# Loads behind the edge exchange, and larger pieces of filler work, in a lattice-and-convolution kernel

## The chip, the core and the metric

The kernel runs on one core of a Trainium2 chip. The metric is the device time of one execution in microseconds (us): 12252.35 us in the median of three runs, from 12244.07 to 12260.76. One more execution was recorded by the hardware profiler; its rows are what the text quotes. Of the core's engines, TensorE (PE, PEld for its weight loads) multiplies matrices, VectorE (DVE), ScalarE (ACT) and GpSimd (POOL) work elementwise, and SyncE (SP) only issues transfers (DMAs), in the order of its queue.

## What is computed

The input x has 32 images of 8 channels of 256 x 256. Two residual layers follow each other:

```python
# layer 0, v = groupnorm(x)
drive = grid = v
for _ in range(15):
    mapped = 3.9 * grid * (1.0 - grid)
    local = conv3x3(mapped, K_local, groups=8)         # each channel for itself
    grid = 0.85 * (0.7 * mapped + 0.3 * local) + 0.15 * drive
cml = clip(grid, 1e-4, 1 - 1e-4)
nca = sigmoid(conv1x1(relu(conv3x3(v, Wp, bp)), Wu, bu))       # 8 -> 128 -> 8 channels
g = sigmoid(conv1x1(relu(conv3x3(concat(v, cml, nca), Wg1, bg1)), Wg2, bg2))
x = x + g * cml + (1 - g) * nca
# layer 1, v = groupnorm(x): both sides quantised to whole numbers up to 127
x = x + conv3x3(q(v), q(weight)) / (sx * sw) + bias
```

## The kernel before

The images are worked on in 8 groups of 4. Layer 0 of a group has four kinds of work, all with TensorE at their centre.

*The lattice* (`lattice`, `half`) iterates `grid`. One channel of four images is a unit; a unit's four images are two pairs, s = 0 and s = 1, and each of the 15 steps does s = 0 and then s = 1. One such piece, 32 matrix products in 64 x 64 quarters of the array and three tiny marks between them (lines 502 and 277), is called a *stretch* here; there are 8 x 8 x 15 x 2 = 1920. A stretch writes two PSUM units; VectorE then takes each half out (`gt`, line 513) and applies the map (line 523), which makes the next step's operand, `m_a` or `m_b`, in SBUF. The image lies over the partitions in overlapping tiles, so that after some steps the rows at the tiles' edges must come from neighbours. Where step + s is even, the stretch reads `m_a`, writes `m_b`, and a small GpSimd product mends the edge (line 528). Where it is odd, it reads `m_b`, writes `m_a`, and two transfers from `m_a` to `m_a` carry the edge rows, 33 KB each: the *exchange* (lines 477 and 478, on SyncE's queue). The next stretch of the same pair s, two stretches later, reads what the exchange brings. No exchange is made in the last step.

*The hidden layer* (`nca`, line 588) makes 128 channels from 8. One *ph pair* is 12 matrix products into one PSUM unit; ScalarE applies the relu (line 596). The 1 x 1 product that follows is the *acc* work: four products at a time (line 604). An image is done in 8 bands t, each with 8 ph pairs and four times four acc products, from an input tile `im` that four transfers of 384 KB fill (line 569), for the next band while this one runs; there are two `im` buffers.

*The gate* (`gate`, line 767) does per band 4 products with the last band's result (line 717) and 40 with two tiles `gin` and `gnc` (three transfers of 384 KB), and takes a third input, `mix` (two transfers of 384 KB, one buffer), to the elementwise end on GpSimd and VectorE. It runs one group behind.

*The preparation* (`normalise`) of the next group's images is small on TensorE.

TensorE's order is that of the program. `together` lays it: after each stretch it takes pieces from the other three kinds, the filler, until the filler's share of its total weight has caught up with the lattice's. The weights are what the generators yield: 2.05 for a stretch, 1.4 for a ph pair, 0.9 for four acc products, 2.3 for a gate batch; the totals stand in `T_NCA`, `T_GATE`, `T_PREP`, `T_LATTICE` (line 896). After each stretch one of the gate's elementwise steps (`chores`) is written too, among them the request for the next `mix`. The other engines and SyncE's queue are ordered by a scheduler with its own estimate of times: a load may be put into the queue anywhere that its buffer and its place in the program allow. All transfers of layer 0 go through SyncE's queue; apart from the loads named above these are the drive's pieces for the next unit (`d_a`, `d_b`, 36 KB and more), the lattice's results, the normalised images and the outputs of hidden layer and gate.

PSUM has three units of two banks for stretches (two each), ph pairs (one) and gate batches (one).

After the last group's lattice and hidden layer come its gates alone, and then layer 1, which the change doesn't touch.

Of the kernel before, what the change touches and what calls it, by code (L numbers as in the profile page):

```python
# [31 lines left out]
F32 = mybir.dt.float32  # L32
# [77 lines left out]
def kernel(  # L110
# [19 lines left out]
    def dram_ap(t, offset, dims):  # L130
        return bass.AP(t.tensor, t.offset + offset, dims)
# [123 lines left out]
    with ExitStack() as one:  # L255
# [139 lines left out]
        def lattice(g):  # L395
# [67 lines left out]
            def background(n):  # L463
# [4 lines left out]
                if g == 0 and units.keys() - {0}:  # L468
                    for _ in range(min(n, len(borders))):
                        nc.sync.dma_start(*borders.pop(0))  # L470

            def exchange(t):

                t = t.rearrange("p (k t) j -> p k (t j)", k=2)
                n = (NT - 1) * (NJ + 2)
                above, below = slice(0, n), slice(NJ + 2, NJ + 2 + n)
                nc.sync.dma_start(t[0::16, :, below], t[14::16, :, above])
                nc.sync.dma_start(t[15::16, :, above], t[1::16, :, below])
# [4 lines left out]
            def half(c, step, s, d, m_a, m_b):  # L483

                a2b = (step + s) % 2 == 0
                n = NJ + 1 if a2b else NJ
                k = 0 if a2b else 1
                two = [unit(), unit()]

                def blocks(j, diagonal, first):  # L490
                    t0, t1 = JOBS[j]
                    pt = two[j // 2][:, j % 2, : (t1 - t0) * n].rearrange("p (t j) -> p t j", j=n)
                    own = m_a[:, t0:t1, 1 : 2 + NJ] if a2b else m_b[:, t0:t1, 0:NJ]
                    beside = m_a[:, t0:t1, 0 : 1 + NJ] if a2b else m_b[:, t0:t1, 1 : 1 + NJ]
                    if diagonal:
                        parts = ((LOW, LOW, k, own), (HIGH, HIGH, k, own))
                    elif a2b:
                        parts = ((LOW, HIGH, k, own), (HIGH, LOW, 2, beside))
                    else:
                        parts = ((HIGH, LOW, k, own), (LOW, HIGH, 2, beside))  # L500
                    for src, dst, w, rhs in parts:
                        T.matmul(pt[dst], lw[src, c, w, dst], rhs[src], start=first, stop=not first)  # L502

                for n_, (o, dg, first) in enumerate(((1, 0, True), (3, 2, True), (0, 1, False), (2, 3, False))):
                    blocks(o, False, first)
                    blocks(dg, True, first)
                    if n_ < len(MARKS):
                        mark(n_)

                gts = []  # L510
                for pt, (ts, w) in zip(two, HALVES):
                    gt = gp.tile([P, 10 * (NJ + 1)], F32, name="gt", tag="gt")[:, : 2 * w * n]
                    V.scalar_tensor_tensor(  # L513
                        gt.rearrange("p (u c) -> p u c", u=2), pt[:, :, : w * n], FLOOR,
                        d[:, ts, :].rearrange("p (u t) j -> p u (t j)", u=2), ALU.max, ALU.add,
                    )
                    gts.append(gt.rearrange("p (t j) -> p t j", j=n))
                for gt, (ts, w) in zip(gts, HALVES):
                    if step == STEPS - 1:
                        V.tensor_scalar(d[:, ts, :], gt, 0.0001, 1.0 - 0.0001, ALU.max, ALU.min)  # L520
                        continue
                    to = m_b[:, ts, :] if a2b else m_a[:, ts, 1 : 1 + NJ]
                    V.scalar_tensor_tensor(to, gt, 1.0, gt, ALU.subtract, ALU.mult)  # L523
                if step == STEPS - 1:
                    return a2b
                if a2b:
                    edge = m_b[:, :, 0 : NJ + 1 : NJ]
                    G.tensor_tensor(edge, edge, junk.unsqueeze(1).to_broadcast([P, TU, 2]), ALU.mult)  # L528
                else:
                    exchange(m_a)  # L530
                return a2b

            if g == 0:
# [5 lines left out]
            for c in range(C):  # L539
                u = g * C + c  # L540
                for step in range(STEPS):
                    if step == 7 and u + 1 < NG * C:
                        units[u + 1], dmas = load(u + 1)
                        later.extend(dmas)
                    if step == STEPS - 1:
                        background(len(later))
                    for s in range(2):
                        d = units[u][s][1 if (step + s) % 2 == 0 else 0]
                        a2b = half(c, step, s, d, m_a[s], m_b[s])
                        if step == STEPS - 1:  # L550
                            for k in range(2):
                                later.extend(store(g * GB + 2 * s + k, c, "b" if a2b else "a", d, k))
                            if u + 1 in units:
                                begin(units[u + 1], s)
                        background(4)
                        yield 2.05

            stored[g] = issued[0] + len(later)
            if g == NG - 1:
                background(len(later))  # L560

        ORDER = ((0, 4, 1, 5), (2, 6, 3, 7))

        def rows(b, t):

            im = ims[(NT8 * b + t) % 2]
            for k in range(2):
                for q in range(2):
                    nc.sync.dma_start(
                        im.bitcast(F32)[64 * q : 64 * q + 48, k, :, 1 : 1 + W],  # L570
                        dram_ap(
                            xp_s[b % NBUF], (32 * t + 16 * k + 8 * q) * ROW, [[W, 48], [ROW, 8], [1, W]]
                        ),
                    )
            return im

        loaded = {}

        def nca(b):
# [19 lines left out]
            pend = done = None  # L599

            def drain():
                acc, t, i, hs = pend
# [20 lines left out]

            ahead = loaded.pop(b, None) or rows(b, 0)
            for t in range(NT8):
                im = ahead
                acc = ps_a.tile([P, 512], F32, name="acc", tag="acc")
                for i in range(4):
                    hs = {}
                    for n in (i, i + 4):  # L630
                        hs[n], hs[n + 8] = hidden([im[64 * q : 64 * q + 48, :, n, :] for q in range(2)])
                        if n == 0:
                            if t < NT8 - 1:
                                ahead = rows(b, t + 1)
# [12 lines left out]
            nc.sync.dma_start(*done)  # L647

        def scales(b):
# [9 lines left out]
        def inputs(b, t):  # L659

            src = gs_s[b % NBUF]
            gin = gip.tile([96, 8, W], F32, name="gin", tag="gin")
            gnc = gip.tile([48, 8, W], F32, name="gnc", tag="gnc")
            for j, to in enumerate((gin[:48], gin[48:], gnc)):
                nc.sync.dma_start(
                    to, dram_ap(src, j * PART + 32 * t * C * W, [[W, 48], [4 * C * W, 8], [1, W]])
                )
            return gin, gnc

        def blend(b, t):  # L670

            src = gs_s[b % NBUF]
            mix = gip.tile([P, 3, 2, W], F32, name="mix", tag="mix", bufs=1)
            for k in range(2):
                nc.sync.dma_start(
                    mix[:, :, k, :],
                    dram_ap(src, (32 * t + 16 * k + 1) * C * W, [[W, P], [PART, 3], [1, W]]),
                )
            return mix

        flat = lambda t: t.rearrange("p k w -> p (k w)")

        def arrange(sc, mix):
# [24 lines left out]
        def gate(b):  # L708
# [38 lines left out]
            for t in range(NT8 + 1):  # L747
# [5 lines left out]
                    now["gt"] = opened(two[:, 1, :], last["r1"])  # L753
                    now["was"] = last
                if t < NT8:
                    (gin, gnc), mix = ahead
# [21 lines left out]
                    was["y"] = mixed(now["gt"], *was["df"])  # L778

                def arrange_(now):  # L780
                    now["df"] = arrange(sc, now["mix"])

                def blend_(now):
                    if now["t"] < NT8 - 1:
# [106 lines left out]
        def after(g, gen):  # L891
# [189 lines left out]
```

## Time and profile before

| | |
|---|---|
| profiled execution | 12231.09 us, of it 12229.3 us span |
| median of the runs | 12252.35 us |
| lattice with filler | to about 11,290 us of the span |
| last gates alone | to about 11,670 us |
| layer 1 | to the end |
| TensorE busy, 1500 to 11,000 us | 8830.18 of 9500 us, granted clock 0.98 |
| VectorE busy, same stretch of time | 6212.55 us |
| DMA engines' busy share, same | 0.70, at 141 GB/s |
| transfers | 1760 MB, of it 896 exchanges of two times 33 KB and 2304 loads of 384 KB |

A line of the page's groups reads: line, engine, operation, output<-inputs, form and count, then busy time and the mean of one in ns, then the idle time of the engine just before these instructions with what ended it. A line of the time order reads: start, duration, engine, line, operation, count, and in brackets the idle time before it with what ended it; PE is TensorE, and SPq is SyncE's queue, where the duration is the issue alone and says nothing of the landing. A line of the time windows reads: from:to, length, busy time (and count) of PE, PEld, DVE, ACT and POOL, then the granted TensorE clock, the DMA engines' busy share and GB/s.

### The profile page before, as it was taken

Reading aid. Unit: us, or ns where it says so; the run is one execution under the profiler, and the core shown is the slowest. Engines: PE = TensorE matmul, PEld = TensorE weight load, DVE = VectorE, ACT = ScalarE, POOL = GpSimd, SP = SyncE. Lnnn points to the kernel's source line nnn. Section 1 sums busy time; section 2 is a strip of 40 time slices with the busy share of each in tenths; the row PEclk is TensorE's granted clock in tenths of the full one; section 3 lists DMA queues with packets and bytes.
Section 4 is the critical chain, followed back from the end, with each engine's and each line's share of the span. In section 5 each row is a group of like instructions: output and inputs, shape, how many; then the busy total and the mean of one; then the engine's idle time right before and its main releaser. Section 6 shows DMA issues by size and latency. Waiting matters only on the chain. (4 is left out here: it accounts for less than half of the span.)

```text
span 12229.3 us, 289998 instructions
## 1 busy us (share of the span) xinstructions
PE 10809.9 (88%) x124192; PEld 6033.0 (49%) x124192; DVE 7826.2 (64%) x11376; ACT 3791.0 (31%) x4034; POOL 1577.2 (13%) x2242
## 2 busy tenths in 40 slices
PE   4888899999999999999999999999999999999854
PEld 2544555555555555555555555555555555554222
DVE  4655666666666666666666666666666666665377
ACT  2222233332333333333333333333333333332133
POOL 1000011111111111111111111111111111111200
PEclk7999999999999999999999999999999999999776
DMA  6545567766777667766776667777677666665988
GB/s 171 97 98 102 101 136 147 143 140 138 147 142 148 137 137 145 151 141 134 148 151 139 135 140 147 143 145 149 133 146 149 141 133 129 126 123 114 204 249 259
DMA packets 2473159, 1759.74 MB, mean 144 GB/s; under 512 B 1021280, under 2 KB 2442944, under 8 KB 2471744
## 3 DMA queue, kind: packets, MB, share of 16 engines
q1 hardware_dynamic: 2380096, 1651.64, 66.0%
q10 hardware_dynamic: 91776, 89.53, 2.3%
q8 instruction: 979, 16.04, 0.6%
q14 instruction: 308, 2.52, 0.1%
HBM read 1130.62 MB, written 473.89 MB: 131 GB/s over the span
## 5 line engine op out<-in xcount | busy, mean ns | idle before, releaser
L596 ACT ACTIVATE h<-pt,bp_sb 128x1024 f32<-128x1024 f32 x2048 | 2275.6, 1113 | 4947.7 <-PE pt L588 4944.3
L588 PE MATMUL pt<-im,wp_hi 48*128 48x512 f32 x12288 | 2631.8, 424 | 165.4 <-ACT h L596 116.6
L502 PE MATMUL pt<-m_a,lw 64*64 64x325 f32 (+1 forms) x30720 | 2299.3, 433 | 464.9 <-DMA m_a<-m_a 410.1
L513 DVE SCALAR_TENSOR_TENSOR gt<-pt,d_b 128x650 f32<-128x650 f32 (+1 forms) x1920 | 1463.5, 763 | 1945.0 <-PE pt L502 1931.7
L588 PE MATMUL pt<-im,wp_lo 48*128 48x512 f32 x12288 | 2442.5, 393 | 0.2 <-issue 0.2
L513 DVE SCALAR_TENSOR_TENSOR gt<-pt,d_a 128x640 f32<-128x640 f32 (+1 forms) x1920 | 1447.2, 754 | 1531.5 <-PE pt L502 1528.2
L502 PE MATMUL pt<-m_b,lw 64*64 64x320 f32 (+1 forms) x30720 | 2200.5, 417 | 118.1 <-DVE gt L513 82.1
L502 PEld LDWEIGHTS pt<-m_a,lw 64*64 64x64 f32 x30720 | 1316.6, 138 | 1193.2 <-issue 596.9
L588 PEld LDWEIGHTS pt<-im,wp_hi 48*128 48x128 f32 x12288 | 1163.6, 185 | 1275.4 <-issue 719.4
L502 PEld LDWEIGHTS pt<-m_b,lw 64*64 64x64 f32 x30720 | 1237.4, 134 | 858.4 <-issue 463.5
L523 DVE SCALAR_TENSOR_TENSOR m_a<-gt 128x640 f32<-128x640 f32 (+1 forms) x1792 | 1431.7, 799 | 58.6
L523 DVE SCALAR_TENSOR_TENSOR m_b<-gt 128x650 f32<-128x650 f32 (+1 forms) x1792 | 1384.6, 774 | 101.3 <-DVE gt L513 2.8
L528 POOL TENSOR_TENSOR m_b<-m_b,junk 128x36 f32<-128x36 f32 x896 | 243.8, 272 | 7994.9 <-DVE m_b L523 5672.1
L588 PEld LDWEIGHTS pt<-im,wp_lo 48*128 48x128 f32 x12288 | 1168.7, 186 | 201.7 <-issue 0.6
L604 PE MATMUL acc<-h,wu_z 128*32 128x512 f32 x8192 | 1107.7, 612 | 0.0
L767 PE MATMUL pt<-gin,gw 96*32 96x384 f32 (+2 forms) x10240 | 772.0, 450 | 201.3 <-ACT gate L719 178.0
L277 PE MATMUL mark<-qw 64*64 64x1 bf16 x5760 | 947.6, 165 | 0.0
L277 PEld LDWEIGHTS <-qw 64*64 64x64 bf16 x5760 | 632.4, 110 | 205.4 <-issue 9.8
L767 PE MATMUL pt<-gnc,gw 48*32 48x126 f32 (+2 forms) x10240 | 733.1, 429 | 0.0
L767 PEld LDWEIGHTS pt<-gin,gw 96*32 96x32 f32 x10240 | 313.8, 115 | 823.7 <-issue 425.2
L690 POOL TENSOR_TENSOR d<-mix 128x256 f32<-128x256 f32 x512 | 552.1, 1095 | 1240.8 <-DVE gate L725 840.1
L767 PEld LDWEIGHTS pt<-gnc,gw 48*32 48x32 f32 x10240 | 295.0, 108 | 420.8 <-issue 415.3
(110 smaller groups left out, 5939.0 us busy)
## 6 DMA issues: line engine op xcount, KB each, us to landing
im<-xp_s SPq DMA_DIRECT2D x1024, 384.0 KB
gin<-gs_s SPq DMA_DIRECT2D x512, 384.0 KB
mix<-gs_s SPq DMA_DIRECT2D x512, 384.0 KB
gnc<-gs_s SPq DMA_DIRECT2D x256, 384.0 KB
d_a<-gs_s SPq DMA_DIRECT2D x2048, 36.0 KB
yb<-y_s ACTq DMA_DIRECT2D x28, 2432.0 KB
xr<-in_x_dram SPq DMA_DIRECT2D x128, 512.0 KB
xp_s<-hi SPq DMA_DIRECT2D x256, 256.0 KB
```

Source lines behind the costliest of these rows:

```text
L277: T.matmul(one_[dst], qw[src, 0, dst], qw[src, 0, 0:1], start=True, stop=True)
L502: T.matmul(pt[dst], lw[src, c, w, dst], rhs[src], start=first, stop=not first)
L513: V.scalar_tensor_tensor(gt.rearrange("p (u c) -> p u c", u=2), pt[:, :, : w * n], FLOOR, d[:, ts, :].rearrange("p (u t) j -> p u (t j)", ...
L523: V.scalar_tensor_tensor(to, gt, 1.0, gt, ALU.subtract, ALU.mult)
L528: G.tensor_tensor(edge, edge, junk.unsqueeze(1).to_broadcast([P, TU, 2]), ALU.mult)
L588: T.matmul(ph[:, i, :].rearrange("p (h w) -> p h w", w=W), w[64 * i : 64 * i + 48, dx, :], rhs[:, :, dx : dx + W], start=(dx == 0 and w is ...
L596: S.activation(h.rearrange("p i c -> p (i c)"), ph.rearrange("p i c -> p (i c)"), AF.Relu, bias=bp_sb)
L604: T.matmul(acc[32 * g : 32 * g + 32], wu_z[:, 24 - 8 * i : 56 - 8 * i], hs[4 * g + i], start=(i == 0), stop=(i == 3),)
L690: G.tensor_tensor(d[:, cols], mix[:, 1, k], mix[:, 2, k], ALU.subtract)
L767: T.matmul(three[32 * i : 32 * i + 32, :, to], gw[:rows_, j, dx, :], src[:, i::4, of], start=(j == 0 and n == 0), stop=(j == 1 and n == le ...
```

## The change

Two things are changed. The large loads (`im`, `gin`, `gnc`, `mix`) are no longer issued where they are requested: a request goes into a list, `asked`. When a stretch makes an exchange, `feed` issues the oldest requests, until 1200 KB are spent (with 384 KB each, up to four), each with an ordering edge that puts it behind the exchange's second transfer in SyncE's queue. Whoever needs a tile whose load was not issued by then issues it himself (`settle`); after the last group's lattice there is no waiting for exchanges (`alone`).

And the filler comes in larger pieces: two ph pairs at a time (weight 2.9), eight acc products at a time after every second of these (1.9), a gate batch with weight 4.5, a stretch with 2.4; the totals follow. The number of products of each kind is the same.

```diff
+            def feed(behind):
+                room = 1200
+                while asked and room > 0:
+                    job = asked.pop(0)
+                    if job[1]:
+                        room -= job[0]
+                        tc.add_manual_dep(begun(job).ins, behind.ins.name, BEHIND, reason="behind the exchange")
+
             def exchange(t):
...
-                nc.sync.dma_start(t[15::16, :, above], t[1::16, :, below])
+                return nc.sync.dma_start(t[15::16, :, above], t[1::16, :, below])
...
-                    exchange(m_a)
+                    feed(exchange(m_a))
...
-                        yield 2.05
+                        yield 2.4
...
             if g == NG - 1:
                 background(len(later))
+                alone.append(True)
+                settle(asked)
...
+        asked, alone = [], []
+        BEHIND = mybir.DependencyInfo(mybir.DependencyClass.NoSync, mybir.DependencyReason.DATA)
+
+        def begun(job):
+            args, job[1] = job[1], None
+            return nc.sync.dma_start(*args)
+
+        def settle(jobs):
+            for job in jobs:
+                if job[1]:
+                    begun(job)
+
+        def ask(jobs):
+            if alone:
+                settle(jobs)
+            else:
+                asked.extend(jobs)
+            return jobs
...
             ahead = loaded.pop(b, None) or rows(b, 0)
             for t in range(NT8):
-                im = ahead
+                im, jobs = ahead
+                settle(jobs)
                 acc = ps_a.tile([P, 512], F32, name="acc", tag="acc")
                 for i in range(4):
                     hs = {}
                     for n in (i, i + 4):
                         hs[n], hs[n + 8] = hidden([im[64 * q : 64 * q + 48, :, n, :] for q in range(2)])
-                        if n == 0:
-                            if t < NT8 - 1:
-                                ahead = rows(b, t + 1)
-                            elif all((b + 1, g) in ready for g in range(4)):
-                                loaded[b + 1] = rows(b + 1, 0)
-                        yield 1.4
-                    if i == 2 and done:
-                        nc.sync.dma_start(*done)
-                        done = None
-                    if pend:
-                        done = drain() or done
-                    pend = (acc, t, i, hs)
-                    yield 0.9
-            done = drain()
-            yield 0.9
+                    pend.append((acc, t, i, hs))
+                    if i == 0:
+                        if t < NT8 - 1:
+                            ahead = rows(b, t + 1)
+                        elif all((b + 1, g) in ready for g in range(4)):
+                            loaded[b + 1] = rows(b + 1, 0)
+                    yield 2.9
+                    if i % 2:
+                        if done:
+                            nc.sync.dma_start(*done)
+                            done = None
+                        while pend:
+                            done = drain(*pend.pop(0))
+                        yield 1.9
...
-                yield 2.3 if t < NT8 else 0.9
+                yield 4.5 if t < NT8 else 0.9
...
-        T_NCA, T_GATE, T_PREP, T_LATTICE = 473.6, 77.2, 4.8, 8 * 30 * 2.05
+        T_NCA, T_GATE, T_PREP, T_LATTICE = 32 * 15.4, 4 * (8 * 4.5 + 0.9), 4.8, 8 * 30 * 2.4
```

`rows`, `inputs` and `blend` return their tiles with the list of requests that `ask` took, instead of issuing the transfers; `gate` and `arrange` call `settle` on it before the tile is first used.

More of the change, by code (lines that the diff above doesn't have):

```diff
@@ L560, in lattice @@
                 background(len(later))
+                alone.append(True)
+                settle(asked)
         ORDER = ((0, 4, 1, 5), (2, 6, 3, 7))
+        asked, alone = [], []
[13 more added lines that the diff above has]
+            return jobs
         def rows(b, t):
             im = ims[(NT8 * b + t) % 2]
[L567 to L572, printed above, removed]
-                        ),
-                    )
-            return im
+            return im, ask(
+                [
+                    [
+                        384,
+                        (
+                            im.bitcast(F32)[64 * q : 64 * q + 48, k, :, 1 : 1 + W],
+                            dram_ap(
+                                xp_s[b % NBUF],
+                                (32 * t + 16 * k + 8 * q) * ROW,
+                                [[W, 48], [ROW, 8], [1, W]],
+                            ),
+                        ),
+                    ]
+                    for k in range(2)
+                    for q in range(2)
+                ]
+            )
         loaded = {}
@@ L597, in hidden, with drain @@
                 return h[:, 0, :], h[:, 1, :]
-            pend = done = None
-            def drain():
-                acc, t, i, hs = pend
+            pend, done = [], None
+            def drain(acc, t, i, hs):
                 for g in range(4):
@@ L663, in inputs @@
             gnc = gip.tile([48, 8, W], F32, name="gnc", tag="gnc")
[L664 to L668, printed above, removed]
+            return gin, gnc, ask(
+                [
+                    [
+                        384,
+                        (to, dram_ap(src, j * PART + 32 * t * C * W, [[W, 48], [4 * C * W, 8], [1, W]])),
+                    ]
+                    for j, to in enumerate((gin[:48], gin[48:], gnc))
+                ]
+            )
         def blend(b, t):
@@ L673, in blend, with arrange @@
             mix = gip.tile([P, 3, 2, W], F32, name="mix", tag="mix", bufs=1)
[L674 to L679, printed above, removed]
+            return mix, ask(
+                [
+                    [
+                        384,
+                        (
+                            mix[:, :, k, :],
+                            dram_ap(src, (32 * t + 16 * k + 1) * C * W, [[W, P], [PART, 3], [1, W]]),
+                        ),
+                    ]
+                    for k in range(2)
+                ]
+            )
         flat = lambda t: t.rearrange("p k w -> p (k w)")
-        def arrange(sc, mix):
+        def arrange(sc, mix, jobs):
+            settle(jobs)
             d = wk.tile([P, 512], F32, name="d", tag="d", bufs=1)
@@ L755, in gate @@
                 if t < NT8:
-                    (gin, gnc), mix = ahead
+                    (gin, gnc, jobs), mix = ahead
+                    settle(jobs)
                     if t < NT8 - 1:
@@ L780, in arrange_ @@
                 def arrange_(now):
-                    now["df"] = arrange(sc, now["mix"])
+                    now["df"] = arrange(sc, *now["mix"])
                 def blend_(now):
```

## The prediction

> **What bounds the kernel now.** I read the page's busy table and slices first, then TensorE's groups, then the waits, then the time order of SyncE and TensorE around one long wait.
>
> ```profile
> span 12229.3 us, 289998 instructions
> ...
> PE 10809.9 (88%) x124192; PEld 6033.0 (49%) x124192; DVE 7826.2 (64%) x11376; ACT 3791.0 (31%) x4034; POOL 1577.2 (13%) x2242
> ...
> PE   4888899999999999999999999999999999999854
> ...
> PEclk7999999999999999999999999999999999999776
> ```
>
> TensorE is busy nine tenths of every slice but the ends, at a clock of 0.9 and more, and its order is written by hand: what it waits is lost. It waits for little, and for one thing most:
>
> ```profile
> L502 PE MATMUL pt<-m_a,lw 64*64 64x325 f32 (+1 forms) x30720 | 2299.3, 433 | 464.9 <-DMA m_a<-m_a 410.1 <-issue 17.4 <-DVE gt L513 14.2
> ```
>
> 410.1 us go to the edge exchange (m_a<-m_a). This is how the longest of them arise. SyncE's queue, then TensorE:
>
> ```profile
> 4022.32 0.64 SPq L477 DMA_DIRECT2D m_a<-m_a  x1
> 4023.00 0.62 SPq L478 DMA_DIRECT2D m_a<-m_a  x1
> 4023.72 1.92 SPq L569 DMA_DIRECT2D im<-xp_s  x4
> 4026.10 0.62 SPq L477 DMA_DIRECT2D m_a<-m_a  x1
> 4026.77 0.61 SPq L478 DMA_DIRECT2D m_a<-m_a  x1
> ```
>
> ```profile
> 4029.57 0.39 PE L588 MATMUL pt<-im,wp_lo 48*128 48x512 f32 x2
> 4036.14 1.79 PE L502 MATMUL pt<-m_a,lw 64*64 64x325 f32 x11 [6.18 <-DMA m_a<-m_a]
> ```
>
> ```profile
> 4023.30:4030.00 6.70, 6.55 (x71) 3.81 (x67) 5.54 (x8) 1.80 (x2) 0.00 (x0) 1.00 0.87 147
> 4030.00:4036.10 6.10, 0.00 (x0) 0.00 (x0) 0.11 (x1) 1.11 (x1) 0.25 (x1) 0.64 1.12 190
> 4036.10:4042.90 6.80, 6.75 (x49) 4.41 (x49) 2.98 (x4) 0.10 (x1) 0.00 (x0) 0.57 0.60 175
> ```
>
> An exchange is made when step + s is odd: by s = 1 of an even step, then by s = 0 of the next step, which is the very next stretch; then not for three stretches. I call them the early and the late exchange. Here four im loads (1.5 MB) went out behind an early one, and the late one stood behind them: its readers waited 6.18 us, and the 6.8 us after the wait ran at a granted clock of 0.57. That is the pattern the change makes a rule of.
>
> **Prices from the trace.** A lattice stretch takes 2.16 us. A lone ph pair lasts 1.59 us to the next kind of work, two in a row 2.97; four acc products 1.00, eight 1.85; a gate batch 1.87 + 5.43. From a stretch's end to the exchange's issue it is 2.69 us in the median (VectorE's four operations), to its landing another 2.35 (its packets, the only ones of 2112 bytes, tell), to the reader's start 0.5: 5.5 in all. With four big loads between early and late exchange (49 times) the late one lands 12.2 us after the first load's issue in the mean, 10.9 at least and 13.3 to 13.5 at most; with the three of gin and gnc 9.0; with two of mix 6 to 7. The first load directly behind an early exchange is issued 1.4 us after it.
>
> **The change, part by part** (counted in the order of both programs).
>
> 1. Larger pieces. Before, 1416 lone and 316 double ph runs: 1416 x 1.59 + 316 x 2.97 = 3190 us; after, 1024 double ones, 3041. Acc: 994 x 1.00 + 15 x 1.85 = 1022; after 512 x 1.85 = 947. Together **-223 us**, on the path.
>
> 2. Fewer pieces than gaps. Stretches back to back rise from 14 to 269. PSUM holds: of three units, the second stretch's second one comes free with the first stretch's gt (0.82 us), as it is needed. But an exchange's reader has less work before it: 154 have under 5.5 us against 32, short by 98 us against 18: **+80 us**. Where the exchange isn't used (m_b edges), VectorE and GpSimd's 0.25 us need some 3.5 us and have 5.1 or more in all but four cases: nothing.
>
> 3. The loads. Before, the long gap between a late exchange and the next early one holds 3.77 big loads in the mean, the short one 1.02, and 313 of 448 short gaps have none. After, 405 of 448 early exchanges have two to four loads directly behind: 178 have four with at least three of im, 49 two of im and two of mix, 71 three, 105 two of mix. Reason: a job waits for the next exchange, and three of four stretches lead to an early one. Of the late ones 222 are followed by three or four; there the next exchange is three stretches away (18 us and more to its reader, where four need 16.8) and nothing is lost. So the waits of today go, **-410 us**, and new ones come. From the early stretch's end to the late exchange's reader the four need 2.69 + 1.4 + 12.2 + 0.5 = 16.8 us. TensorE has two stretches and three gaps there: in 124 of the 178 cases 12.1 us, in 48 only 9.1. Short: 974 us. The 49 mixed ones have 15.4 and lack 69; three loads need 13.6 and lack 53; two lack nothing. **+1095 us**; with 11.0 for four loads (and 8.2 for three) 801, with 13.3 (and 10.0) 1395. Check against today: the ten cases directly behind an early exchange with one pair in each gap have 10.1 to 10.8 and so lack 6.0 to 6.7; measured waits are 5.8 to 8.1.
> What stands behind these loads in SyncE's queue: the late exchange itself, held by their issue (0.5 us each, over before it is due), and stores, for which nobody on TensorE waits soon. The im loads land 4.8 us or more before their use by the same count, so they are covered.
>
> 4. The clock. All 43 TensorE waits of 3 us and more between 300 and 11,250 us are followed by half clock; 3 to 5 us by 3.9 us of busy time at half speed, 5 to 7 by 4.5, longer ones by 4.8, which costs half of that. New: 124 + 6 x 2.0, 48 x 2.4, and 0.35 each for the 120 short ones: +417. Today 356 us of busy time at half clock follow the lattice's waits (188 those of 3 us and more, 100 those of 2 to 3, 68 those of 1 to 2), which costs 178; they go: **+239 us**.
> [...]
>
> 5. VectorE, ScalarE and GpSimd do the same work in about the same order (GMGM, gt and m by turns, in 1542 of 1792 stretches against 1547). The waits of ph for ScalarE and VectorE (145 us today) I leave as they are, plus or minus 100: two ph pairs in a row take a unit each, freed by the stretch before. Of the last-group gates and the second layer, 11,290 us on, nothing changes.
>
> Sum: 12,231 (profiled execution, 21 us under the median of the runs) - 223 + 80 - 410 + 1095 + 239 = 13,012; on the median's scale 13,033. I say **13,030 us**, 6% slower.
>
> **Rivals.**
> *The loads are gone before the late exchange is due (faster).* The short gap is not always short: with a gate in it there are 16 us. If four loads took 9 us instead of 12.2, 13.6 would be needed: 124 x 1.5 + 48 x 4.5 = 402, clock about 140, and 12,231 - 223 + 80 - 410 + 402 + 140 - 178 = 12,042. It turns at about 9.7 us; the lowest of 49 is 10.9. If the late exchange went past the loads altogether, 11,500. Against it: 9.1 us of landing time in the mean with four loads ahead, 2.46 with none.
> *The waits come, but no slower clock,* because TensorE is denser otherwise: 12,231 - 223 + 80 - 410 + 1095 - 178 = 12,595. Against it: 43 of 43.
> *More than summed:* 13.3 us per four loads, as with im loads in the trace's slower half, gives 1395 and 2.4 of clock each: 13,370. For it: in the stalls the queue also carries stores.
> *A load whose buffer isn't free blocks SyncE and with it the late exchange.* Mix waits for GpSimd today 78 times, 92 us; 413 mix loads now stand directly behind early exchanges. Were each of these 206 pairs held as long as those, 1.2 us: +250. For it: one buffer. Against: the request is made a stretch after the work that reads it.
> *The grouping does nothing,* since pieces are equal: +223 on the sum, 13,235.
>
> **How the numbers follow.** Waits and clock as summed, give or take the landing time: 0.60 (12,750 to 13,400). Waits without most of the clock's part, or landing times near 11: 0.25 (12,450 to 12,750). Above 13,400: 0.05. Faster: 0.07; within 0.2% (what a measurement can tell from no change): 0.03. The range 12,450 to 13,400 leaves out about 0.15.
>
> **What would show it.** In the profile after: TensorE's wait for m_a<-m_a some 1000 to 1300 us against 410.1, over 150 of them above 3 us; TensorE's busy share under 0.85 and its clock near 0.95 in the middle, against 0.98 between 1500 and 11,000 us today; im loads directly behind the first exchange of a pair; ph groups in twos, fewer weight-load gaps. I am wrong if the late exchange lands within 5 us behind four loads, or if other waits, such as VectorE's on a shorter TensorE order, take over.

## The result, and the profile after

The changed kernel takes 13162.18 us (median of the runs, 13151.4 to 13174.35) against 12256.56 us: a ratio of 1.0738, with a 95% interval of 1.0719 to 1.0757. The profiled execution took 13174.35 us, 943 us more than that of before.

The page, with its busy table and the slices of TensorE and of its clock:

```profile
span 13172.6 us, 289701 instructions
...
PE 10954.0 (83%) x124192; PEld 6357.5 (48%) x124192; DVE 7736.0 (59%) x11376; ACT 3800.8 (29%) x4034; POOL 1583.7 (12%) x2242
...
PE   4888888888888888888888888888888888888854
...
PEclk9999999998999999999999989998999989999777
```

The engines do what they did, but TensorE stands at eight tenths where it stood at nine, and four slices of the clock between the ends show an 8, where there was none. TensorE's groups, sorted by busy time, say what it waits for:

```profile
L626 PE MATMUL pt<-im,wp_hi 48*128 48x512 f32 x12288 | 2615.6, 420 | 129.2 <-DVE gt L522 106.3 <-DMA im<-xp_s 17.5 <-DVE rstd_y L882 4.7
L511 PE MATMUL pt<-m_a,lw 64*64 64x325 f32 (+1 forms) x30720 | 2548.8, 471 | 1328.5 <-DMA m_a<-m_a 1293.2 <-issue 20.9 <-ACT h L634 10.4
```

1293.2 us go to the edge exchange, where it was 410.1, and the same products last 471 ns instead of 433. The wait for the ph products' own loads stays small (17.5 us, 18.1 before). One of the new waits, in the time order of SyncE's queue and of TensorE, and in the time windows (length, busy time of PE, PEld, DVE, ACT, POOL, then clock, DMA share, GB/s):

```profile
6817.12 0.64 SPq L486 DMA_DIRECT2D m_a<-m_a  x1
6817.81 0.63 SPq L487 DMA_DIRECT2D m_a<-m_a  x1
6818.49 1.97 SPq L580 DMA_DIRECT2D im<-xp_s  x4
6822.23 0.62 SPq L486 DMA_DIRECT2D m_a<-m_a  x1
6822.90 0.61 SPq L487 DMA_DIRECT2D m_a<-m_a  x1
6823.55 0.99 SPq L580 DMA_DIRECT2D gin<-gs_s  x2
```

```profile
6826.20 0.40 PE L626 MATMUL pt<-im,wp_lo 48*128 48x512 f32 x2
6832.00 1.36 PE L511 MATMUL pt<-m_a,lw 64*64 64x325 f32 x8 [5.40 <-DMA m_a<-m_a]
```

```profile
6818.00:6826.60 8.60, 8.60 (x106) 4.94 (x98) 5.92 (x8) 1.87 (x2) 0.11 (x1) 1.00 0.95 145
6826.60:6832.00 5.40, 0.00 (x0) 0.03 (x1) 0.00 (x0) 1.11 (x1) 0.14 (x1) 0.71 1.13 152
6832.00:6838.80 6.80, 6.80 (x59) 4.66 (x59) 2.98 (x4) 1.01 (x1) 0.04 (x1) 0.73 1.09 196
```

It is the pattern of before: four im loads behind the early exchange, the late one behind them, 5.40 us of waiting, and then products at a clock of 0.73. What was an accident every now and then has become the rule: over the lattice, from 300 us on, 183 waits of TensorE are 3 us and longer.

To compare the kernels I split the lattice stage (from the first ph product to the last lattice product) of each trace into four sums: TensorE's waits for the exchange, its other waits, the loss by the clock (half of the time that it was busy at half clock; there the first eight products of a stretch that reads `m_a` take 1.11 us in the changed kernel, and 0.60 at full clock, both medians), and the rest, which is the work at full clock. The 957 us after that stage are 959 after.

| us | exchange | other waits | clock | work | stage |
|---|---|---|---|---|---|
| before | 411 | 477 | 222 | 9973 | 11,082 |
| after | 1294 | 378 | 549 | 9805 | 12,026 |
| difference | +883 | -99 | +327 | -168 | +943 |

### The profile page after: what moved, and what is told of

It reads as the page before. It is cut to its first block, busy times and chain, and to the rows that moved or that the text cites. A ratio compares the mean times of both kernels' runs of the same rounds, so it can differ in the third digit from the quotient of the medians.

```text
span 13172.6 us, 289701 instructions
## 1 busy us (share of the span) xinstructions
PE 10954.0 (83%) x124192; PEld 6357.5 (48%) x124192; DVE 7736.0 (59%) x11376; ACT 3800.8 (29%) x4034; POOL 1583.7 (12%) x2242
## 4 chain that ended last, share of the span: by engine, by line
PE 64%; DMA 22%; DVE 6%; SPq 2%; issue 2%; ACT 2%; ACTq 1%; POOL 0%; POOLq 0%; DVEq 0%
PE pt L511 28%; PE pt L626 17%; DMA m_a<-m_a 16%; PE pt L817 11%; PE acc L641 5%; DVE gt L522 3%; DMA yb<-y_s 3%; PE pt L766 2%; ACT gate L768 1%; SPq L486 1%; DVE m_a L532 1%; ACTq L1051 1%; DMA gin<-gs_s 1%; ACT h L634 1%; SPq L465 0%
## 5 line engine op out<-in xcount | busy, mean ns | idle before, releaser
L511 PE MATMUL pt<-m_a,lw 64*64 64x325 f32 (+1 forms) x30720 | 2548.8, 471 | 1328.5 <-DMA m_a<-m_a 1293.2
L511 PEld LDWEIGHTS pt<-m_a,lw 64*64 64x64 f32 x30720 | 1494.9, 150 | 2248.1 <-issue 1343.3
L626 PE MATMUL pt<-im,wp_lo 48*128 48x512 f32 x12288 | 2486.0, 399 | 0.0
L511 PE MATMUL pt<-m_b,lw 64*64 64x320 f32 (+1 forms) x30720 | 2171.2, 413 | 35.1 <-ACT h L634 28.9
L626 PEld LDWEIGHTS pt<-im,wp_hi 48*128 48x128 f32 x12288 | 1197.7, 190 | 798.4 <-issue 277.7
L626 PEld LDWEIGHTS pt<-im,wp_lo 48*128 48x128 f32 x12288 | 1200.2, 190 | 224.4
L641 PE MATMUL acc<-h,wu_z 128*32 128x512 f32 x8192 | 1031.0, 600 | 6.0 <-ACT h L634 6.0
L817 PE MATMUL pt<-gnc,gw 48*32 48x384 f32 (+2 forms) x10240 | 745.6, 435 | 0.5 <-DMA gnc<-gs_s 0.5
L739 POOL TENSOR_TENSOR d<-mix 128x256 f32<-128x256 f32 x512 | 519.5, 1027 | 1100.6 <-DMA mix<-gs_s 818.3
```

The lines of the kernel that those rows point to most:

```text
L626: T.matmul(ph[:, i, :].rearrange("p (h w) -> p h w", w=W), w[64 * i : 64 * i + 48, dx, :], rhs[:, :, dx : dx + W], start=(dx == 0 and w is ...
L641: T.matmul(acc[32 * g : 32 * g + 32], wu_z[:, 24 - 8 * i : 56 - 8 * i], hs[4 * g + i], start=(i == 0), stop=(i == 3),)
L739: G.tensor_tensor(d[:, cols], mix[:, 1, k], mix[:, 2, k], ALU.subtract)
L817: T.matmul(three[32 * i : 32 * i + 32, :, to], gw[:rows_, j, dx, :], src[:, i::4, of], start=(j == 0 and n == 0), stop=(j == 1 and n == le ...
```

## The experiments

The same sums for every kernel that was run; the ratio is that to the kernel before on the same chip, with its 95% interval:

| run | exchange | other waits | clock | work | median us | ratio |
|---|---|---|---|---|---|---|
| e2_pieces_only | 524 | 484 | 344 | 9824 | 12311.33 | 1.0025 to 1.0054 |
| e3_loads_only | 928 | 441 | 487 | 9969 | 12968.87 | 1.0546 to 1.0593 |
| e4_warm | 522 | 416 | 251 | 10,666 | 12983.33 | 1.0558 to 1.0613 |
| e1_split | 823 | 437 | 419 | 9814 | 12616.29 | 1.0264 to 1.0308 |
| e7_dose3 | 941 | 395 | 544 | 9802 | 12802.30 | 1.0428 to 1.0474 |
| e12_split42 | 557 | 741 | 617 | 9816 | 12875.62 | 1.0477 to 1.0522 |
| e5_before_actq | 659 | 763 | 546 | 9974 | 13119.09 | 1.0690 to 1.0733 |
| e6_pieces_actq | 841 | 828 | 577 | 9824 | 13195.43 | 1.0745 to 1.0794 |
| e8_hold_small | 339 | 480 | 259 | 9967 | 12187.58 | 0.9928 to 0.9961 |
| e9_hold_large | 473 | 435 | 293 | 9825 | 12171.01 | 0.9920 to 0.9950 |
| e10_hold2_small | 480 | 456 | 269 | 9965 | 12304.45 | 1.0027 to 1.0059 |
| e11_hold2_large | 694 | 464 | 443 | 9816 | 12536.13 | 1.0216 to 1.0251 |

**Each part alone.** The first keeps the larger pieces and issues every load where it is requested; the second keeps the loads behind the exchanges and takes the pieces and weights of before.

```diff
 def ask(jobs):                     # e2_pieces_only
-    if alone:
-        settle(jobs)
-    else:
-        asked.extend(jobs)
+    settle(jobs)
     return jobs
```

```diff
-yield 2.9                          # e3_loads_only: hidden layer
+yield 1.4
...
-yield 4.5 if t < NT8 else 0.9      # gate
+yield 2.3 if t < NT8 else 0.9
...
-yield 2.4                          # stretch
+yield 2.05
...
-T_NCA, T_GATE, T_PREP, T_LATTICE = 32 * 15.4, 4 * (8 * 4.5 + 0.9), 4.8, 8 * 30 * 2.4
+T_NCA, T_GATE, T_PREP, T_LATTICE = 473.6, 77.2, 4.8, 8 * 30 * 2.05
```

> The larger pieces alone; each load is issued where it is requested, as before. In this order only 25 early exchanges have four loads behind them before the late one (after: 229). Theory: 223 us of switching gone, 80 us of shorter chains added, waits for the exchange about as before: 12,110 us (11,950 to 12,250). Rival (the pieces cost): near 13,000 us.

> The loads behind the exchange alone, with the pieces and weights of before. 260 early exchanges have four loads directly behind, but with small pieces TensorE has 0.9 us more work on the average up to the late exchange's reader; short by 771 us by the same count as in the prediction (after: 1095). Theory: 12,257 - 410 + 790 + 150 of clock = 12,790 us (12,500 to 13,000). Rival (pieces cost, loads don't): 12,250 us or less.

The loads alone cost 5.7% of the 7.4, inside what was expected, and so are the main cause. The pieces alone were expected to gain and lost 0.4%. Their saving is there (work 9973 to 9824, that is 149 us), but the exchange costs 113 us more and the clock 122. The group of the lattice's products in e2_pieces_only:

```profile
L511 PE MATMUL pt<-m_a,lw 64*64 64x325 f32 (+1 forms) x30720 | 2370.7, 445 | 562.6 <-DMA m_a<-m_a 523.9 <-issue 23.7 <-ACT h L631 6.9
```

Counted exchange by exchange (all idle time of TensorE in the stretch that reads it, so that the sums lie up to 20 us above those of the table), the late ones wait less (262 us before, 187 here), and the early ones more (168, and 355): 89 of these come after seven loads in the long gap and cost 262 us, where before there were 21 with 32 us. The pieces change where requests fall, not only how long pieces take. On top of the loads behind the exchange they make the kernel 193 us slower (e3_loads_only to the changed kernel), although they save 164 us of work there: the exchange's wait rises from 928 to 1294.

**Is the clock part real?** 28 useless products of 384 columns are put in front of each lattice stretch that reads a late exchange issued behind three or more im loads, so that TensorE works where it waited.

```diff
+if s == 0 and (c, step) in heavy:
+    warm = ps_m.tile([P, 384], F32, name="mark", tag="mark")
+    for _ in range(28):
+        T.matmul(warm, qw[:, 0, :], qw.rearrange("p d m -> p (d m)"), start=True, stop=True)
```

> The kernel after, and ahead of each stretch that reads a late exchange whose early one had three or four im loads behind it, 28 bf16 products of 384 columns on the whole array, some 4.6 us, that nothing uses: TensorE does them while it would wait. If the clock's fall in the wait costs what the prediction says (about 2 us each), the time falls by 200 to 350 us to some 12,880 us though work is added; the waits for the exchange fall to some 450 us and the busy time at half clock to 400 us. If the clock costs nothing by itself: 13,160 us or a little more.

The 28 products are busy for 4.72 us a time (845.6 us in 179 stretches). 861 us of added work (10,666 less 9805) made the kernel 179 us faster. Exchange wait and added work together are 1383 us, no less than the 1294 of waiting before them, so no transfer came sooner; the clock's loss fell from 549 to 251. That a wait costs more than its length because the clock drops behind it is thereby shown, at some 300 us here. The windows of the middle, first of the changed kernel, then of e4_warm (the clock is the third number from the end):

```profile
1500.00:12000.00 10500.00, 9093.73 (x105796) 5319.37 (x105791) 6201.30 (x9338) 3055.47 (x3177) 1325.58 (x1864) 0.93 0.64 128
```

```profile
1500.00:12000.00 10500.00, 9686.75 (x111406) 5657.36 (x111408) 6283.56 (x9439) 3085.39 (x3212) 1340.21 (x1887) 0.98 0.65 130
```

**How many loads behind the early exchange.** `feed` gets its budget as an argument. e1_split lets two loads go behind an early exchange and five behind a late one, e7_dose3 three and four; e12_split42, tried later, two and four.

```diff
-def feed(behind):
-    room = 1200
+def feed(behind, room):
...
-feed(exchange(m_a))
+feed(exchange(m_a), 1900 if step % 2 else 400)     # e1_split
+feed(exchange(m_a), 1200 if step % 2 else 800)     # e7_dose3
+feed(exchange(m_a), 1200 if step % 2 else 400)     # e12_split42
```

> Both changes stay, but at most two loads go directly behind an early exchange, and up to five behind a late one (after: up to four behind each). Theory (four loads behind the early exchange make the late one late, and the clock falls in the wait): two loads need 10.6 us, which nearly every late exchange's reader has; TensorE's wait for the exchange falls from 1293 us to some 250, busy time at half clock from 1028 us to some 300, and the time to 13,162 - 1040 - 360 = 11,760 us (11,600 to 11,950), under the kernel before. Rival (fewer, larger pieces are what costs, by stretches back to back): 12,900 us or more, since the pieces stay. Rival (any ordering of loads behind exchanges jams SyncE's queue): 12,500 us or more.

> The kernel after, with at most three loads behind an early exchange instead of four (up to four behind a late one stay). By the count of the prediction 306 early exchanges have three, short by 461 us (four: 1103; two: 71). If the number of loads ahead of the late exchange sets the loss, the time lies between the run with two, 12,616 us, and the one with four, 13,162 us: 12,800 us (12,680 to 12,920), with waits for the exchange of some 1000 us. If the order alone costs, however many they are: 13,100 us or more.

With two, three and four loads behind the early exchange the time is 12,616, 12,802 and 13,162 us, and the late exchange costs 0.7, 2.5 and 5.0 us a case, so the dose does act. The time of e7_dose3 was met; its three loads, though, cost 764 us in 306 cases, where the count before the run had 461. And e1_split missed its 11,760 us by far. 300 us of its exchange wait still stand with the late exchanges behind two loads (404 cases), and 436 with the early ones behind five (210 cases), where the prediction had put nothing. Those land fast, 2.63 us after their issue; they are issued late: 119 early exchanges that go out more than 4 us after their stretch hold 459 us of idle time, all the other early ones 46. SyncE's queue of e1_split around one, with the row of VectorE that makes the operand ready, and the reader:

```profile
6041.26 1.98 SPq L579 DMA_DIRECT2D im<-xp_s  x4
6043.28 0.47 SPq L579 DMA_DIRECT2D gin<-gs_s  x1
6043.80 13.56 SPq L465 DMA_DIRECT2D gs_s<-d_b  x8
6057.40 1.75 SPq L465 DMA_DIRECT2D gs_s<-d_a  x4
6059.25 0.39 SPq L678 DMA_DIRECT2D gs_s<-nca  x1
6059.75 0.67 SPq L485 DMA_DIRECT2D m_a<-m_a  x1
```

```profile
6053.92 0.69 DVE L531 SCALAR_TENSOR_TENSOR m_a<-gt 128x512 f32<-128x512 f32 x1
```

```profile
6062.59 1.79 PE L510 MATMUL pt<-m_a,lw 64*64 64x325 f32 x11 [3.61 <-DMA m_a<-m_a]
```

The operand was there at 6054.61, the exchange went out at 6059.75. Between the five loads and the exchange stand small transfers of line 465; eight of them take 13.56 us from the first issue to the last, where the next four take 1.75. The last five of the eight are issued at 6046.10, 6048.77, 6051.65, 6054.44 and 6056.66, each within 0.02 us of the landing of one of the five loads. SyncE's own waits of e1_split give the sum for im:

```profile
SPq L465 <- DMA im<-xp_s: 561.1, 338, 3.8
```

A small transfer waits, before it may be issued, until an im load has landed, and all that is behind it in the queue waits too. (The last five of the eight small transfers stand eight places behind the five loads. In the changed kernel 926 of SyncE's 10,324 transfers from 300 us to the end of the lattice go out, after a wait, within 0.15 us of the landing of the one eight places before.) Before, this wait was 294.0 us, 171 times, and in the changed kernel it is 797.0, 427 times, so its sum alone does not tell the damage; what counts is whether an exchange stands behind it. 251 exchanges of e1_split go out more than 4 us after their stretch, 147 in the changed kernel, 82 before. So a late side with many loads is not free: they do not delay the exchange's landing but its issue.

> As the run with at most two loads behind an early and five behind a late exchange (12,616 us, exchange 823 us), but four behind a late one. In that run 436 us of the wait fell on early exchanges after five loads, which landed as fast as ever (2.6 us) but were issued late; after four, in the run with three and four, the 216 early ones lost 106 us. Theory (SyncE's queue jams behind the fifth load): 310 us of exchange wait and some 150 of clock go, time 12,150 us (12,050 to 12,300). Rival (the two loads behind the early exchange, or the sum of all loads, are what costs): 12,500 us or more.

This one missed its 12,150 us by 726 and shows the limit on the other side. With four behind the late exchange the jam shrinks (the early exchanges that go out more than 4 us late hold 202 us, 459 in e1_split) and the exchange's wait falls to 557 us, near what was expected. But now the loads themselves come late: six may go per pair of exchanges, where some five are asked for in the mean (2304 over 448 pairs). TensorE's waits for transfers other than the exchange rise from 18 us in e1_split to 360 (the first line below holds 223.3 of them), GpSimd's for mix from 796.0 to 1897.5, and the clock loses 617.

```profile
L816 PE MATMUL pt<-gnc,gw 48*32 48x384 f32 (+2 forms) x10240 | 906.0, 508 | 223.3 <-DMA gnc<-gs_s 223.3
```

```profile
POOL d L738 <- DMA mix<-gs_s: 1897.5, 232, 18.6
```

**Is it the queue's order, or the loads on whatever queue?** The loads go on ScalarE's queue, the exchange stays on SyncE's; once in the kernel before, once with the larger pieces, the loads issued where they are requested.

```diff
-nc.sync.dma_start(...)      # im, gin, gnc, mix
+nc.scalar.dma_start(...)
```

> The kernel before, with the four kinds of large loads issued on ScalarE's queue instead of SyncE's; nothing else. Theory (a late exchange is late because its packets stand behind the loads' in the same queue, or its issue behind theirs): loads in another queue cannot hold it; TensorE's waits for the exchange fall from 411 us to 150 or less, the clock's loss from 222 to some 110, and the time by some 370 us to 11,880 us (11,750 to 12,050), less what ScalarE loses by issuing 2304 loads of 0.5 us. Rival (the loads take the DMA engines' time, whatever their queue): waits for the exchange stay at 400 us or more, time 12,250 us or more. Rival (ScalarE becomes the bound: its relu comes late behind issues and their waits): TensorE's waits for ScalarE rise from 328 us by several hundred.

> The larger pieces, and the large loads where they are requested, on ScalarE's queue (against the run with the pieces alone, 12,311 us, one thing differs: the loads' queue). Theory: waits for the exchange fall from 524 us to some 180 (100 of it by the chains that the larger pieces shorten), the clock's loss from 344 to 150: 11,770 us (11,600 to 11,950), and so under the one with small pieces on the same queue by some 100 us. Rival (DMA engines shared, queue no matter): 12,300 us.

Both missed by 1200 us and more, and with them fell the theory that only the order in one queue matters. The mean landing time of an exchange in us after its issue, by the number of loads issued in the 5 us before it (cases in brackets):

| | none | two | three | four |
|---|---|---|---|---|
| loads on the same queue, before | 2.81 | 3.84 (71) | 5.84 (33) | 8.87 (68) |
| loads on the same queue, after | 2.46 | 2.72 (74) | 4.18 (55) | 9.36 (177) |
| loads on the same queue, e2_pieces_only | 2.81 | 5.26 (21) | 7.32 (10) | 8.59 (27) |
| loads on ScalarE's queue, e5_before_actq | 2.63 | 5.80 (82) | 6.75 (61) | 5.93 (50) |
| loads on ScalarE's queue, e6_pieces_actq | 3.35 | 4.40 (133) | 4.78 (40) | 5.63 (122) |

Behind four loads the exchange lands some 3 us sooner when the queues differ (e5_before_actq against before, e6_pieces_actq against e2_pieces_only), which is about half of the delay. Behind two and three it lands sooner in the second of these pairs and later in the first. So the order in one queue is part of the delay, the rest stays when the queues differ, and how large each part is, is not shown: the loads' places in time changed with the queue. The 5.9 and 5.6 us behind four loads lie between the 2.6 and 3.4 with none and the 8.9 and 8.6 on the same queue; by what the loads hold the exchange up from another queue is not shown. Nothing steered the loads away from the exchanges any more, and the other waits rose as well, to 763 and 828 us, against 477 before and 484 in e2_pieces_only. SyncE was no freer either; from its waits in e5_before_actq:

```profile
SPq L737 <- DVE y L726: 805.1, 176, 18.8
...
SPq L465 <- DMA im<-xp_s: 444.6, 166, 7.5
SPq L465 <- DMA gin<-gs_s: 438.3, 180, 6.9
```

TensorE's waits for ScalarE, which now has 2304 transfers to issue, rose from 328 to 470 us in e5_before_actq, against 248 us more for the exchange and 324 more by the clock; what ScalarE's later work did beyond that was not measured apart.

**Loads out of the short gap only.** A request made between an early and a late exchange is held and issued behind the late one; any other is issued at once, with no budget. e8_hold_small does this with the pieces of before, e9_hold_large with the larger ones.

```diff
+short = [False]
 def feed(behind, late):
-    room = 1200
-    while asked and room > 0:
+    short[:] = [not late]
+    while late and asked:
...
 def ask(jobs):
-    if alone:
+    if alone or not short[0]:
         settle(jobs)
...
-feed(exchange(m_a))
+feed(exchange(m_a), step % 2 == 1)
```

> The kernel before, with small pieces and its loads issued where they are requested, but for one rule: a load requested between an early and a late exchange waits for the late one and goes behind it. So no early exchange has more than two loads behind it before the late one (before: 49 with four, 61 with three). Theory: TensorE's waits for the exchange fall by those cases' 220 us from 411 to some 230 us, the clock's loss from 222 to some 140, time 12,250 - 180 - 80 = 11,990 us (11,900 to 12,130), under the kernel before. Rival (held loads only shift the wait to the next exchange or jam SyncE's queue): 12,230 us or more.

> The same rule with the larger pieces (the run with the pieces alone: 12,311 us, exchange 524 us, 25 cases of four loads in the short gap). Theory: 140 us of those go, and 50 of clock; the waits of early exchanges, that loads late in the long gap hold up (262 us), stay: 12,130 us (12,020 to 12,250). Rival as above: 12,300 us.

Both are faster than both kernels: 0.55% and 0.65% under the kernel before, with intervals that overlap, so the pieces are worth little or nothing here (17 us between the medians). In e8_hold_small the late exchanges' wait falls from 262 us to 17, as meant; but that of the early ones rises from 168 to 345, and a quarter of the expected gain is left. Most of the rise is late issue again: early exchanges that go out more than 4 us after their stretch hold 181 us (92 cases), 27 before (45). The group in e9_hold_large:

```profile
L510 PE MATMUL pt<-m_a,lw 64*64 64x325 f32 (+1 forms) x30720 | 2359.6, 443 | 514.3 <-DMA m_a<-m_a 472.1 <-issue 19.8 <-DVE gt L521 10.3
```

230 of these 472.1 us stand with 84 early exchanges that come after seven loads in the long gap.

To be rid of these, requests made from the stretch before the early exchange on were held too:

```diff
+if s == 0 and step % 2 == 0 and step < STEPS - 1:
+    short[:] = [True]
```

> Small pieces; loads requested in the stretch ahead of an early exchange are held too, till behind the late one. No exchange has loads close ahead of it, but 49 late ones have seven loads directly behind, 77 five or six. If closeness of loads alone counted: exchange 120 us and 11,850 us. As the runs showed that SyncE's queue jams behind five loads (early exchanges issued up to 11 us late): 250 us at these, and 12,050 us (11,900 to 12,250).

> The same with the larger pieces: 51 late exchanges with seven loads behind them, 53 with five or six, and the chains shorter. 12,150 us (11,950 to 12,350); where the queue doesn't jam, 11,850 us.

Both missed. Exchanges land faster in the mean (2.77 and 2.86 us, 3.48 before), yet the wait went up, to 480 and 694 us: 243 and 202 exchanges are issued more than 4 us after their stretch, and the early ones among them hold 427 and 314 us. Five to nine loads in one go bring back e1_split's jam. In e11_hold2_large another 229 us stand with 66 early exchanges that are issued in time and land slowly.

## Why the prediction was right, and which terms were off

The forecast was 13,030 us, in a range of 12,450 to 13,400; it came to 13,162. Against the profiled execution it summed +781 us, and the lattice stage got 943 longer. Step by step:

1. *Larger pieces*, -223: the work at full clock fell by 168, alone by 149. The mechanism is right and the size a third too large. Two ph pairs last some 3.0 us and eight acc products 1.85, as priced. Two stretches back to back, which come 255 times, are not what is missing: such a pair takes 4.37 us in the median, and twice 2.16 is 4.32. Where the other 55 us went is not shown. "The grouping does nothing" fell, and so did my trust that its saving would be kept: alone it loses (e2_pieces_only).

2 and 3. *The exchange*, +80 - 410 + 1095 = +765: it came to +883. The late exchanges with four loads behind the early one are 229 (178 and 49 were counted), and cost 1139 us (974 and 69). From the first load's issue the late one lands after 12.1 us in the mean, 12.2 was taken. The 71 with three loads cost 36 (53 predicted); those with two or none 37, and the early ones 96. So the count from the program's order held nearly to the case, and a chain of four measured durations against the work that TensorE has meanwhile gave the wait within a tenth.
Some of that is luck. The cases with three or four im loads (180) cost 1112 us against 974, the 49 with two of im and two of mix 27 against 69. And in the 180 the reader starts 1.3 us after the exchange's last packet, where 0.5 was taken, and TensorE has 12.1 us of work in the mean, where the count came to some 11.3: two misses of 0.8 us that cancel. The rest of the chain (issue, first load, landing) lies 0.7 us a case above its prices.
The sentence that the issue of the loads is "over before it is due" was a little off: over all exchanges the issue comes 3.37 us after the stretch in the mean, 2.99 before. That three or four loads behind a late exchange lose nothing is about right (the 222 early exchanges after them wait 39 us in all) and does not carry to five, as e1_split showed. The prediction had no step for it: it named SyncE blocked by a busy buffer as a rival. That wait fell (a mix load waits for GpSimd 43 times, 62 us, where it was 78 times, 92); what blocks SyncE is a load that hasn't landed (small transfers waited 427 times for an im load, 797 us).

4. *The clock*, +417 - 178 = +239: it came to +327. Here each interval of half clock is put down to the longest wait of TensorE around its start, and half of TensorE's busy time in it is its cost:

| half clock behind, us | before | after |
|---|---|---|
| waits of 3 us and more, all the lattice's | 94 | 414 |
| the lattice's waits of 1 to 3 us | 71 | 25 |
| ph's waits of 1 to 3 us | 34 | 54 |
| the rest | 17 | 53 |

Of the 417, 375 were for 178 new waits of 3 us and more; 183 came, 181 of them followed by half clock, and they cost 414. That today's costs behind the lattice's waits "go" held: the long waits of after are the new ones, and the short ones cost 25, where 42 were reckoned. The term that failed is the one put at nothing: the sum took only the lattice's waits, and half clock behind ph's waits and the rest costs 56 us more than before. Why is not shown.
Half clock comes in multiples of 3.4 us here: 52 intervals of one, 124 of two, 34 of three, 15 of four, and a few longer. Two is the commonest, and the 414 us behind the 183 long waits, 2.3 us each, bear out the price taken from the rows (375 for 178, 2.1 each).

5. *Everything else*, 0 with 100 either way: -99, within it. Waits for ScalarE fell from 328 to 240 us. That this made up for part of the misses above is luck.

Of the rivals, "the loads are gone before the late exchange is due" asked for 9.7 us from the first load to the landing; it was 12.1. That the waits come "but no slower clock" is excluded by e4_warm. "More than summed" named the right side for a wrong reason: the landing time was as priced. The 162 us over the sum are 118 of exchange (96 of it behind four loads), 88 of clock and 55 of smaller saving, less 99 of other waits. What the profile was to show it shows: 1293 us of exchange wait (1000 to 1300), 183 waits above 3 us (over 150), TensorE at 0.83 (under 0.85), a clock of 0.93 in the middle (near 0.95).

## What to carry to other kernels

Before loads are tied to an event, count how long the next thing behind them in that queue has until its reader is due, and whether the load's landing time fits: here three or four loads cost 39 us of waiting behind 222 late exchanges, and four cost 1139 us behind 229 early ones. Spread them as well, since a burst in a safe place can still hold up the issuing engine itself (459 us of idle time at 119 exchanges issued late in e1_split), and a budget that is too small makes them late (360 us of TensorE's waits in e12_split42, 18 in e1_split). The best that was found (0.65% faster) holds back only the loads that would fall into the short gap. And price a wait on TensorE with the half clock behind it, here 2.3 us in the mean on each of 3 us or longer.

## What the runs showed of the hardware

- In the changed kernel an exchange (two transfers of 33 KB) issued within 5 us behind four loads of 384 KB lands after 9.4 us instead of 2.5. Behind three it is 4.2 there and 6.4 in e7_dose3 (mostly im), behind two 2.7 there and 4.3 in e12_split42. On another queue than the loads it is still 5.6 to 5.9 behind four, and 4.4 to 5.8 behind two.
- An engine that issues transfers can be held up by loads that it issued itself: behind five im and gin loads the issue of eight small transfers lasted 13.56 us in e1_split, the last five each waiting for a load's landing.
- Filling a wait with useless products can pay: 861 us of them took the place of 772 us of waiting, gave back 298 us of clock and made this kernel 179 us faster.
